# The experts' stage of a decoder layer, divided into 32 units and laid under a selective scan as a third chain

## The chip, the cores and the metric

The kernel runs on one core of one Trainium2 chip. The metric is the device time of one execution in microseconds (us). Everything is computed in float32. In the lines of the profile PE is TensorE (PEld its weight loads), DVE is VectorE, ACT is ScalarE, POOL is GpSimd and SP is SyncE, on whose queue all transfers are issued. L392 is line 392 of the kernel before.

## What is computed

One post-norm decoder layer on a batch of 32 sequences of 256 tokens of 256 features: a selective scan (Mamba), cross attention to a context with 16 heads of 16, and eight experts with gated feed-forward nets; after each a residual and a layer norm.

```python
x = layernorm(x + mamba(x))
x = layernorm(x + cross_attention(x, ctx))
x = layernorm(x + experts(x))

def mamba(x):
    xc, res = split(x @ W_in.T + b_in)                 # 512 and 512 channels
    u = silu(causal_conv3(xc) + conv_b)
    dlt, Bm, Cm = split(u @ W_x.T)                     # 64, 16, 16
    delta = softplus(dlt @ W_dt.T + b_dt)
    # in chunks of 64 tokens, for 512 channels x 16 states
    h[t] = exp(delta[t] * A) * h[t-1] + delta[t] * Bm[t] * u[t]
    y[t] = sum_n(h[t] * Cm[t])
    return (y * silu(res)) @ W_out.T + b_out

def experts(x):            # expert e has tokens 32 e .. 32 e + 31 of every sequence
    h = silu(x[e] @ w1[e]) * (x[e] @ w3[e])            # 256 -> 704
    return h @ w2[e]                                   # 704 -> 256
```

## The kernel before, and what sets its order

The work is done in two stages.

The first stage holds the scan and the attention of all 32 batches, in an order written out by hand: `tc.manual_schedule()` (L74) makes each engine execute its instructions in the order in which the Python code issues them. The main loop (L617 to L649) runs over steps. Sixteen steps make a batch (`NBLK`), each of 32 channels with 16 states; the 512 pairs of a step lie on 128 partitions and four rows of 256 tokens. The step number within the batch is called k here. A step consists of

- `load_step` (L326), the broadcast load of delta and delta times u for a step that lies `AHEAD` = 5 steps on;
- `decay` (L354), four exponentials on ACT, for the step after next, into one of three `da` buffers;
- `inject` (L368), one product on DVE into `bu`, with `b_bc`, which `spread_b` (L345) has PE write once a batch;
- `recur` (L378), the scan proper on DVE, into one of seven `h` buffers;
- `weigh` (L389), one product with C on POOL;
- after every fourth step `reduce` (L394), 32 matmul instructions on PE that sum over the states into `y`, and three steps later `gate` (L414) on DVE.

Between these, two chains run as Python generators, and `run` takes one of them on by one yield:

- `pre(b + 1)` (L224), called `nxt` in the loop: everything that the scan of the next batch needs. Transposes, `ps_in`, convolution, SiLU, `ps_x`, `ps_dt`, softplus (Abs, Relu, Exp and Ln on ACT, the rest on POOL), and the stores `dd` from which the steps load.
- `attn(b - 1)` (L420), called `prev`: output product of the scan, residual, norm, then the attention. Its parts are the scores `s` (L481) with 16 maxima on DVE (L495), `ps_m`, the subtraction of the maxima in `qT` (L507), the scores again in the other orientation with Exp (L564), `attend` (`ps_oT`, L522), `divide` (`ps_oB`, L540), output product `ps_o`, residual, norm, and the store into `x2d` in HBM. It begins at k=3 of the batch that follows its own.

All products of this stage take their place in PSUM from one pool of five banks, `bank` (L192). A product waits on the chip when its bank hasn't been read. Scores take four banks at once.

The second stage (L654 to L757) begins when the first has ended. Its order is not fixed by hand. It runs over the eight experts; the tokens of an expert from all 32 sequences are 1024 columns, taken in two halves of 512. For each half `up` (L686) forms w1 and w3 products, 512 columns wide, with SiLU on ACT from PSUM and the product on DVE; `down` (L708) forms the product with w2, residual, norm and store. Weights are loaded once for each expert, an expert ahead, into pools of two buffers. A float32 product is two matmul instructions in the profile.

Of the kernel before, what the change touches and what calls it, by code (L numbers as in the profile page):

```python
# [15 lines left out]
P = 128  # L16
# [12 lines left out]
AHEAD = 5  # L29
H, DK = 16, 16  # L30
NG = 4
E, FF = 8, 704
NFC = 6
CT = L // E
EPS = 1e-5
# [3 lines left out]
def decoder_kernel(ctx: ExitStack, tc: tile.TileContext, a: dict, out: bass.AP):  # L39
# [12 lines left out]
    def layernorm(pool, tiles):  # L52
# [7 lines left out]
        yield  # L60
        rstd = pool.tile([P, n, 1], F32, tag="ln_rstd", name="ln_rstd")
# [4 lines left out]
        nc.gpsimd.tensor_scalar_mul(off, off, -1.0)  # L66
        yield
# [5 lines left out]
    with ExitStack() as ph:  # L73
# [6 lines left out]
        esp = ph.enter_context(tc.tile_pool(name="esp", bufs=6))  # L80
        ldp = ph.enter_context(tc.tile_pool(name="ldp", bufs=AHEAD + 1))
        hp = ph.enter_context(tc.tile_pool(name="hp", bufs=7))
# [3 lines left out]
        ps_mm = ph.enter_context(tc.tile_pool(name="ps_mm", bufs=5, space=PSUM))  # L86
# [54 lines left out]
        b_v = column_v = wp.tile([P, 2, 1], F32, name="b_v")  # L141
# [49 lines left out]

        def bank(name):  # L192
            return ps_mm.tile([P, 2 * L], F32, tag="mm", name=name)
# [30 lines left out]
        def pre(b):  # L224

            ps = transposes(xs[b])
# [3 lines left out]
            nc.gpsimd.tensor_tensor(  # L230
                xs[b], xs[b], b_out.unsqueeze(1).to_broadcast([P, 2, D]), ALU.add
            )
# [10 lines left out]

            pss = [project(m2) for m2 in range(2)]
            yield
            for c in range(NDC):
                nc.scalar.activation(  # L247
                    xpad[:, c, 2:], pss[c // 2][:, c % 2], AF.Identity, bias=b_in[:, c : c + 1]
                )
            pss = [project(m2) for m2 in range(2, 4)]  # L250
# [3 lines left out]
            for c in range(NDC):  # L254
                m = NDC + c
                nc.scalar.activation(
                    sres[:, c, :], pss[c // 2][:, c % 2], AF.Identity, bias=b_in[:, m : m + 1]
                )
            pss = [
# [8 lines left out]

            nc.scalar.activation(sres, sres, AF.Silu)
            u = unit1.tile([P, NDC, L], F32, tag="u", name=f"u_{b}")  # L270
            for c in range(NDC):
                nc.scalar.activation(
                    u[:, c, :], pss[c // 2][:, c % 2], AF.Silu, bias=conv_b[:, c : c + 1]
                )
            yield
            ps = bank("ps_x")[:, :L]
# [7 lines left out]
            nc.scalar.copy(xp[:R], ps[:R])  # L284
            xps[b] = xp
            bcds[b] = bcd.tile([NS, L], F32, tag="bcd", name=f"bcd_{b}")
            nc.sync.dma_start(bcds[b], xp[DTR + NS : R])
            yield
            pss = [
# [10 lines left out]
            e = unit1.tile([P, NDC, L], F32, tag="e", name=f"ez_{b}")  # L300
            for dst, f in ((e, AF.Abs), (z, AF.Relu)):
                for c in range(NDC):
                    nc.scalar.activation(
                        dst[:, c, :], pss[c // 2][:, c % 2], f, bias=b_dt[:, c : c + 1]
                    )
            yield
            nc.scalar.activation(e, e, AF.Exp, scale=-1.0)
            lw = unit1.tile([P, NDC, L], F32, tag="lw", name=f"lw_{b}")
            nc.scalar.activation(lw, e, AF.Ln, bias=1.0)
            yield  # L310
            nc.gpsimd.tensor_tensor(z, z, lw, ALU.add)

            nc.gpsimd.tensor_scalar(lw, e, 1.0, -1.0, op0=ALU.add, op1=ALU.add)
            yield
            nc.gpsimd.tensor_tensor(e, e, lw, ALU.subtract)
            nc.gpsimd.tensor_tensor(z, z, e, ALU.add)
            yield
# [96 lines left out]
        def gate(i, y):  # L414
            b, c = i // NBLK, i % NBLK // NJ
            if c == 0:
                ygs[b] = unit1.tile([P, NDC, L], F32, tag="yg", name=f"yg_{b}")
            nc.vector.tensor_tensor(ygs[b][:, c, :], y, sress[b][:, c, :], ALU.mult)

        def attn(b):  # L420

            yg = ygs.pop(b)
            ctxT = cts.pop(b)
            ps_out = product(
# [21 lines left out]
            nc.vector.tensor_tensor(x1, ps_out, xs.pop(b), ALU.add)  # L446
            norm = layernorm(small, [x1[:, t, :] for t in range(2)])
            next(norm)
            kT = unit1.tile([P, NG, L], F32, tag="kT", name=f"kT_{b}")
            biased(kT, b_k, pss)  # L450
            yield
            next(norm)
            ps = product(
# [5 lines left out]
            next(norm, None)  # L459
            nc.scalar.copy(v[:, :, :, :DK], ps.rearrange("p t (h d) -> p t h d", d=DK))  # L460
            yield
# [4 lines left out]
            nc.gpsimd.tensor_tensor(x1, x1, b_o.unsqueeze(1).to_broadcast([P, 2, D]), ALU.add)  # L466
            yield
            pss = [project(w_q, x1T, g2) for g2 in range(2)]
            yield
            qT = unit1.tile([P, NG, L], F32, tag="qT", name=f"qT_{b}")  # L470
            biased(qT, b_q, pss)
            yield
# [18 lines left out]
            for g in range(NG):  # L491
                ss = scores(g, qT, kT)
# [3 lines left out]
            yield  # L496
# [8 lines left out]
            for g2, ps in enumerate(pss):  # L505
# [3 lines left out]
                )  # L509
            yield  # L510
            att = unit1.tile([P, 2, H, DK], F32, tag="att", name=f"att_{b}")
            HH = H // 2
            oT = None

            def attend(g, ess):

                nonlocal oT
                if g % 2 == 0:
                    oT = bank("ps_oT").rearrange("p (g n) -> p g n", g=2)
                for k in range(2):  # L520
                    for j in range(4):
                        nc.tensor.matmul(  # L522
                            oT[32 * j : 32 * j + 32, g % 2, :],
# [6 lines left out]
                        )  # L530

            def divide(g2, oT):

                oS = unit1.tile([P, 2, L], F32, tag="oS", name="oS")
                nc.scalar.copy(oS, oT)
                yield
                ps = bank("ps_oB").rearrange("p (t j n) -> p t j n", t=2, j=2)
                for t in range(2):
                    for j in range(2):
                        nc.tensor.transpose(  # L540
                            ps[:, t, j, :], oS[:, j, t * P : (t + 1) * P], ident
                        )
                yield
# [8 lines left out]
                )  # L552

            last, div = None, iter(())
            for g in range(NG + 1):
                if g < NG:
                    ss = scores(g, kT, qT)
                yield
                next(div, None)
                ess = []  # L560
                if g < NG:
                    for s in ss:
                        es = esp.tile([P, 2, L], F32, tag="es", name="es")
                        nc.scalar.activation(es, s, AF.Exp, scale=1.0 / DK**0.5)  # L564
                        ess.append(es)
                if last is not None:
                    attend(g - 1, last)
                    if g == 2:
                        div = divide(0, oT)
                last = ess  # L570
                yield
                next(div, None)
            for _ in div:
# [248 lines left out]
```

## Time and profile before

| | |
|---|---|
| time, median of 3 runs | 3479.11 us (3478.74 to 3484.37) |
| profiled execution | 3480.61 us, of which its span is 3478.9 us |
| PE busy | 2870.0 us, 82% of the span, 17284 matmuls |
| DVE busy | 2424.9 us, 70% |
| ACT busy | 1980.8 us, 57% |
| POOL busy | 1838.7 us, 53% |
| DMA | 377.10 MB, 108 GB/s over the span |
| mean granted clock of PE | 0.861 |

Busy time is the time in which an engine has an instruction under way. Matmuls are pipelined and their ends are modelled, so PE can be shown busy while it isn't at its peak. The granted clock is the share of the full PE clock that the chip allows at the time. An idle time is put down to the work whose end released the engine.

The costliest groups of the first stage are the product with C (L392, POOL, 512 times 2361 ns), the scan (L380, DVE, 512 times 2285 ns), the decays (L361, ACT, 2048 times 504 ns), `bu` (L371, DVE, 512 times 1222 ns) and the scores (L481, PE).

### The profile page before, as it was taken

What the parts mean: (1) busy time and instruction counts of PE and PEld (TensorE: products, weight loads), DVE (VectorE), ACT (ScalarE), POOL (GpSimd) and SP (SyncE); (2) the same over time, 40 slices, a digit from 0 to 9 for tenths busy, and PEclk for the clock granted to TensorE, in tenths of its full rate; (3) what the DMA queues carried; (4) which work ended last, traced back from release to release, by engine and by line L of the source; (5) the groups of instructions that cost most, each with busy time, mean ns of one, the idle gap of its engine ahead of it and who ended that gap; (6) DMA issues with size and microseconds to landing.
All of it is one profiled execution on the core that took longest, in us unless ns stands there. A gap on an engine that the chain in (4) does not pass through costs nothing. (4 is left out here: it accounts for less than half of the span.)

```text
span 3478.9 us, 47890 instructions
## 1 busy us (share of the span) xinstructions
PE 2870.0 (82%) x17284; PEld 1904.1 (55%) x17284; DVE 2424.9 (70%) x2447; ACT 1980.8 (57%) x4227; POOL 1838.7 (53%) x1143
## 2 busy tenths in 40 slices
PE   2378888888888888888888888888888787999998
PEld 2255555555555555555555555555555553555554
DVE  0578888888888888888888888888888872222222
ACT  1566666666666666666666666666666642121211
POOL 0666666666666666666666666666666640000001
PEclk9678888888888888888888888888888887999999
DMA  2554444444444444444444444444444422221320
GB/s 47 138 132 124 125 122 122 123 125 125 124 126 125 124 122 122 122 122 122 123 125 123 122 122 122 122 122 122 122 122 122 121 59 78 60 62 49 76 52 22
DMA packets 260158, 377.10 MB, mean 108 GB/s; under 512 B 34576, under 2 KB 123920, under 8 KB 259920
## 3 DMA queue, kind: packets, MB, share of 16 engines
q1 hardware_dynamic: 259920, 374.03, 39.5%
q8 instruction: 136, 2.23, 0.3%
q14 instruction: 102, 0.84, 0.1%
HBM read 323.08 MB, written 50.86 MB: 107 GB/s over the span
## 5 line engine op out<-in xcount | busy, mean ns | idle before, releaser
L392 POOL TENSOR_TENSOR h<-h,c_bc 128x1024 f32<-128x1024 f32 x512 | 1208.8, 2361 | 722.4 <-DVE h L380 645.1
L380 DVE TENSOR_TENSOR_SCAN h<-da,bu 128x1024 f32<-128x1024 f32 x512 | 1169.8, 2285 | 61.8 <-ACT da L361 6.3
L361 ACT ACTIVATE da<-ld,a_neg 128x252 f32<-128x252 f32 x2048 | 867.9, 504 | 534.7 <-DVE h L380 514.2
L371 DVE TENSOR_TENSOR bu<-ld,b_bc 128x1024 f32<-128x1024 f32 x512 | 625.6, 1222 | 58.4 <-DMA ld<-dd 49.3
L481 PE MATMUL s<-kT,qT 32*128 32x256 f32 x2048 | 401.1, 667 | 225.8 <-ACT qT L439 176.4
L495 DVE TENSOR_REDUCE mpad<-s 128x2 f32<-128x512 f32 x512 | 316.7, 681 | 280.0 <-PE s L481 280.0
L481 PEld LDWEIGHTS s<-kT,qT 32*128 32x128 f32 x2048 | 278.5, 310 | 338.0 <-ACT qT L439 188.9
L564 ACT ACTIVATE es<-s 128x512 f32<-128x512 f32 x512 | 270.5, 614 | 114.2 <-PE s L481 68.7
L62 POOL TENSOR_SCALAR ln_rstd<-ln_mv 128x2 f32<-128x2 f32 x96 | 21.8, 228 | 592.5 <-DVE ln_mv L59 589.9
L401 PE MATMUL y<-h,sel_y 128*32 128x256 f32 x4096 | 312.8, 453 | 22.9 <-POOL h L392 22.9
L481 PE MATMUL s<-qT,kT 32*128 32x256 f32 x2048 | 280.5, 454 | 43.4 <-ACT es L564 28.9
L705 DVE TENSOR_TENSOR h_ff<-sg,pu 128x512 f32<-128x512 f32 x96 | 65.9, 686 | 294.6 <-PE pu L696 294.6
L217 PE MATMUL ps_in<-xT,w_in 128*128 128x256 f32 x1024 | 243.8, 393 | 24.6 <-ACT xT L229 24.6
L481 PEld LDWEIGHTS s<-qT,kT 32*128 32x128 f32 x2048 | 169.9, 206 | 165.8 <-ACT es L564 106.6
L401 PEld LDWEIGHTS y<-h,sel_y 128*32 128x32 f32 x4096 | 142.8, 128 | 166.5 <-issue 89.4
L217 PEld LDWEIGHTS ps_in<-xT,w_in 128*128 128x128 f32 x1024 | 193.8, 194 | 70.2 <-ACT xT L229 32.7
L716 PE MATMUL po<-w,h_ff 128*128 128x256 f32 (+1 forms) x768 | 193.0, 396 | 0.0
L704 ACT ACTIVATE sg<-pg 128x512 f32<-128x512 f32 x96 | 57.2, 596 | 235.4 <-PE pg L696 235.4
L217 PE MATMUL ps_conv<-xpad,taps 128*128 128x256 f32 x768 | 173.0, 381 | 21.5 <-ACT xpad L247 21.5
L696 PE MATMUL pg<-x2T,w 128*128 128x512 f32 (+1 forms) x384 | 182.1, 596 | 0.0
L696 PE MATMUL pu<-x2T,w 128*128 128x512 f32 (+1 forms) x384 | 180.4, 592 | 0.0
L522 PE MATMUL ps_oT<-es,v 128*32 128x256 f32 x2048 | 154.9, 424 | 24.1 <-ACT es L564 24.1
(100 smaller groups left out, 3786.1 us busy)
## 6 DMA issues: line engine op xcount, KB each, us to landing
ld<-dd SPq DMA_DIRECT2D x1024, 256.0 KB, 4.1
dd<-delta SPq DMA_DIRECT2D x32, 512.0 KB, 2.9
dd<-u SPq DMA_DIRECT2D x32, 512.0 KB, 3.2
w<-in_w SPq DMA_DIRECT2D x16, 704.0 KB, 4.8
x<-in_x SPq DMA_DIRECT2D x32, 256.0 KB, 4.2
c_bc<-bcd SPq DMA_DIRECT2D x64, 128.0 KB, 3.4
ctxT<-in_ctxT SPq DMA_DIRECT2D x32, 256.0 KB, 4.7
x2d<-x SPq DMA_DIRECT2D x32, 256.0 KB, 2.1
```

Of the source, the lines that this page charges most:

```text
L217: nc.tensor.matmul(ps[:, j, :], l, r, start=(k == 0), stop=(k == len(terms) - 1))
L361: nc.scalar.activation(da[:, g, q].rearrange("p (k t) -> p k t", t=CHUNK)[:, :, 1:], loads[i][:, 0, g].rearrange("p (k t) -> p k t", t=CHU ...
L371: nc.vector.tensor_tensor(bu, loads.pop(i)[:, 1].unsqueeze(2).to_broadcast([P, GB, NQ, L]), b_bcs[i // NBLK].unsqueeze(1).to_broadcast([P, ...
L380: nc.vector.tensor_tensor_scan(h.rearrange("p g q t -> p (g q t)"), das_of.pop(i).rearrange("p g q t -> p (g q t)"), bus.pop(i).rearrange( ...
L392: nc.gpsimd.tensor_tensor(hs[i], hs[i], c_bc, ALU.mult)
L401: nc.tensor.matmul(y[32 * j : 32 * j + 32, :], sel_y[:, g, :], hs[i - NJ + 1 + j][:, g, q, :], start=(g == 0 and q == 0), stop=(g == GB - ...
L481: nc.tensor.matmul(ss[j][:, t, :], left[r : r + 32, g, t * P : (t + 1) * P], right[r : r + 32, g, :], start=True, stop=True,)
L495: nc.vector.tensor_reduce(mpad[:, :, g, 32 * j + DK], s, AX.X, ALU.max)
L522: nc.tensor.matmul(oT[32 * j : 32 * j + 32, g % 2, :], v[:, k, 4 * g + j, :], ess[j][:, k, :], start=(k == 0), stop=(k == 1), tile_positio ...
L564: nc.scalar.activation(es, s, AF.Exp, scale=1.0 / DK**0.5)
L696: nc.tensor.matmul(ps[:m], w[:, k, f * P : f * P + m], x2T[:, k, cols], start=(k == 0), stop=(k == 1),)
L716: nc.tensor.matmul(ps[:, j, :], h[:m, f, t * P : (t + 1) * P], w2[:m, f, :], start=(f == 0), stop=(f == NFC - 1),)
```

## The change

The second stage is removed. Its work is divided into 32 units, each of four sequences and two experts, 128 tokens for each expert: unit u takes sequences 4 (u // 4) to 4 (u // 4) + 3 and experts 2 (u % 4) and 2 (u % 4) + 1. The units run one after the other in a generator, `units`, which the main loop takes on as a third chain, twice in each step (`expert_step`). Unit u begins when its four sequences are stored in `x2d` and the loop has reached step 6 of batch u + 5 (`LAG`). What is left after the last step runs behind the loop, alternating with the last attention.

A unit loads `xe` (tokens of both experts) and the first expert's w2, transposes, and forms the w1 products for both experts in three banks of four tiles of 704 / 128; ACT copies them into `h`. Then it loads w3 into the buffers that held w1, and yields `HOLD`: it is taken on only by the call in `pre` just ahead of the SiLU there, so that its own SiLU, over all of `h` in SBUF, stands beside that one. The w3 products follow, with a product on DVE for each bank, then `ps_down` with w2 of the first expert, the load of the second expert's w2 into the same buffer and of the next unit's w1, the second half of `ps_down`, residual, norm and store.

`live`, `take` and `done` count the banks of PSUM while the order is made: a chain that wants banks yields until that many of five are not in use in the order so far, instead of issuing a product that would wait on the chip.

```diff
-AHEAD = 5
+AHEAD = 4
+HBUFS = 6
+RING = 5
+GE = P // CT
+UNITS = B // GE * (E // 2)
+LAG = 5
...
+        def take(n):
+            nonlocal live
+            while live + n > RING:
+                yield
+            live += n
+        def done(n):
+            nonlocal live
+            live -= n
...
+            expert_step(True)
             nc.scalar.activation(sres, sres, AF.Silu)
...
+        def load_w13(u, which, e):
+            t = fw.tile([P, 2, FF], F32, tag="w13", name=f"{which}_{u}_{e}")
+            src = a[which][2 * (u % 4) + e].rearrange("(k p) f -> p k f", p=P)
+            nc.sync.dma_start(t, src)
+            w13s[u, which, e] = t
...
+        def expert_unit(u):
+            yield
+            yield
+            xe = xes.pop(u)
+            yield from take(1)
+            ps = bank("ps_xe").rearrange("p (k e n) -> p k e n", k=2, e=2)
+            for k in range(2):
+                for e in range(2):
+                    nc.tensor.transpose(ps[:, k, e, :], xe[:, e, k * P : (k + 1) * P], ident)
+            yield
+            x2T = unit1.tile([P, 2, 2, P], F32, tag="x2T", name=f"x2T_{u}")
+            nc.scalar.copy(x2T, ps)
+            done(1)
+            yield
+            def hidden(which, b):
+                ps = bank("ps_h").rearrange("p (i n) -> p i n", i=4)
+                for i in range(4):
+                    e, f = FS[4 * b + i]
+                    m = min(P, FF - f * P)
+                    for k in range(2):
+                        nc.tensor.matmul(
+                            ps[:m, i, :],
+                            w13s[u, which, e][:, k, f * P : f * P + m],
+                            x2T[:, k, e, :],
+                            start=(k == 0),
+                            stop=(k == 1),
+                        )
+                return ps
...
+            for b in range(3):
+                yield from take(1)
+                ps = hidden("w1", b)
+                yield
+                for m, i, j in parts(b):
+                    nc.scalar.copy(h[:m, 4 * b + i : 4 * b + j, :], ps[:m, i:j, :])
+                done(1)
+                yield
+            for e in range(2):
+                load_w13(u, "w3", e)
+            yield HOLD
+            nc.scalar.activation(h[:, :FULL, :], h[:, :FULL, :], AF.Silu)
+            nc.scalar.activation(h[:REST, FULL:, :], h[:REST, FULL:, :], AF.Silu)
+            yield
+            for b in range(3):
+                yield from take(1)
+                ps = hidden("w3", b)
+                yield
+                yield
+                for m, i, j in parts(b):
+                    at_ = h[:m, 4 * b + i : 4 * b + j, :]
+                    nc.vector.tensor_tensor(at_, at_, ps[:m, i:j, :], ALU.mult)
+                done(1)
+            yield from take(1)
+            po = bank("ps_down").rearrange("p (e n) -> p e n", e=2)
+            for e in range(2):
+                terms = [i for i in range(len(FS)) if FS[i][0] == e]
...
+                yield
+                if e == 0:
+                    load_w2(u, 1)
+                    if u + 1 < UNITS:
+                        for ee in range(2):
+                            load_w13(u + 1, "w1", ee)
+                    yield
+            nc.vector.tensor_tensor(xe, po, xe, ALU.add)
+            done(1)
+            for _ in layernorm(small, [xe[:, e, :] for e in range(2)]):
+                yield
+            yield
+            for e in range(2):
+                nc.sync.dma_start(rows_of(out, u, e), xe[:, e, :])
+
+        def units():
+            for u in range(UNITS):
+                while stored <= u // 4 * GE + GE - 1 or i < (u + LAG) * NBLK + 6:
+                    yield
+                load_xe(u)
+                load_w2(u, 0)
+                yield from expert_unit(u)
...
+        def expert_step(on_hold=False):
+            nonlocal held
+            if held == on_hold:
+                held = next(unit, None) is HOLD
```

The main loop, after the change, in its new parts:

```diff
             run(prev)
+            expert_step()
             if i < STEPS:
+                if len(hs) == HBUFS:
+                    drain(sums)
                 recur(i)
             run(nxt)
             run(prev)
             if i < STEPS:
                 weigh(i)
-            for f in later.pop(i, ()):
-                f()
+            run(sums)
             if i % NJ == NJ - 1 and i < STEPS:
-                at(i + 2, lambda i=i: summed(i))
-            run(prev if k % 2 else nxt)
-            if k == 3 and b:
-                for _ in prev:
-                    pass
+                drain(sums)
+                sums = summed(i)
+            if b == LAG and k == 0:
+                for e in range(2):
+                    load_w13(0, "w1", e)
+            expert_step()
+            run(prev)
+            if k % 2 == 0:
+                run(nxt)
+                run(prev)
+            if b + 1 == B and k == 3:
+                expert_step(True)
+            if k == 4 and b:
+                drain(prev)
                 prev = attn(b - 1)
-        for _ in prev:
-            pass
+        i = 10**6
+        for _ in unit:
+            run(prev)
```

In the two old chains `take` and `done` stand around every product, and steps are moved apart: `layernorm` yields twice where it yielded once, `pre` issues the residual's bias on POOL a step later, Abs and Relu alternate, and softplus is done in two halves in buffers of half the size (`halves`). The scores, the second scores together with `attend`, and `divide` are each a step of their own; `oT` takes a bank for each group of four heads and is copied in four halves. Attention begins at k=4 instead of k=3. Room in SBUF comes from `AHEAD` 4, six `h` buffers (`HBUFS`), four `es` instead of six, and buffers that are shared (`oS` and `aT` use that of `x1T`, the second residual is written over `x1`); `yg` has two buffers.

## The prediction

> **What bounds the kernel now.** The profiled execution took 3480.61 us, its span 3478.9, so 1.7 us lie around the span; the median of the runs is 3479.11. I make the sum against the span. First I read the busy time by stretches (bounds, length, then busy us of PE, its weight loads, DVE, ACT, POOL; granted clock, DMA share, GB/s), to part the scan from the experts' stage.
>
> ```profile
> 176.00:2728.00 2552.00, 2122.87 (x14356) 1486.03 (x14356) 2118.64 (x1997) 1725.95 (x3726) 1647.54 (x916) 0.85 0.45 123
> ...
> 2920.00:3479.00 559.00, 541.66 (x1664) 285.43 (x1664) 119.06 (x256) 109.90 (x193) 43.51 (x128) 0.99 0.23 59
> ```
>
> The scan is not full on any engine: PE 83%, DVE 83%, ACT 68%. The experts' stage is PE alone at full clock. The batches' `b_bc` products (L349) start at 81.1 us for the first and 2771.5 for the last, that is 86.8 a batch; from 1992.11 to 2770.63 nine batches took 86.5 each.
>
> Next the timeline of one batch. DVE (start, duration, group):
>
> ```profile
> 1512.26 2.29 DVE L380 TENSOR_TENSOR_SCAN h<-da,bu 128x1024 f32<-128x1024 f32 x1
> ...
> 1523.47 2.49 DVE L495 TENSOR_REDUCE mpad<-s 128x2 f32<-128x512 f32 x4 [8.92 <-PE s L481]
> ...
> 1539.67 1.26 DVE L507 TENSOR_TENSOR qT<-qT,ps_m 128x512 f32<-128x512 f32 x2
> ```
>
> Scans and their `bu` follow without a gap until 1514.55; then DVE stands 8.9 us before the reduction of the first scores. PE in the same batch:
>
> ```profile
> 1511.76 3.72 PE L217 MATMUL ps_qk<-x1T,w_q 128*128 128x256 f32 x16 [0.68 <-ACT x1T L465]
> ...
> 1521.36 6.13 PE L481 MATMUL s<-kT,qT 32*128 32x256 f32 x34 [5.88 <-ACT qT L439]
> ...
> 1562.02 0.44 PE L208 MATMUL ps_tr<-ident,att 128*128 128x128 f32 x2 [1.89 <-DVE att L547]
> ...
> 1576.92 5.35 PE L217 MATMUL ps_conv<-xpad,taps 128*128 128x256 f32 x24
> ...
> 1582.10 3.62 PE L217 MATMUL ps_out<-w_out,yg 128*128 128x256 f32 x16
> ...
> 1585.56 3.62 PE L217 MATMUL ps_qk<-ctxT,w_k 128*128 128x256 f32 x16
> ```
>
> PE has the queries at 1515.5, and the scores begin only at 1521.36, after a stop of 5.9 us. Then PE works nearly without a pause from 1562 (transposes of `att`) to the next queries. ACT says why the scores wait:
>
> ```profile
> 1514.46 1.11 ACT L307 ACTIVATE ez<-ez 128x1024 f32<-128x1024 f32 x1
> ...
> 1515.60 1.28 ACT L309 ACT_TABLE_LOAD   x1
> ...
> 1520.86 1.54 ACT L439 ACTIVATE qT<-ps_qk,b_q 128x256 f32<-128x256 f32 x4
> ```
>
> `qT` is behind softplus and its tables. The granted clock in short windows (the column after POOL) is what the stop costs afterwards:
>
> ```profile
> 1516.00:1520.00 4.00, 0.00 (x0) 0.00 (x0) 0.00 (x0) 3.96 (x5) 1.98 (x1) 0.79 0.00 0
> ...
> 1520.00:1524.00 4.00, 2.64 (x18) 2.08 (x18) 0.53 (x1) 3.97 (x11) 3.91 (x2) 0.50 0.00 0
> ...
> 1562.00:1566.00 4.00, 3.98 (x12) 3.27 (x13) 3.78 (x3) 2.28 (x5) 2.10 (x2) 0.58 0.69 192
> ...
> 1582.00:1586.00 4.00, 4.00 (x21) 3.51 (x20) 2.58 (x3) 3.97 (x7) 2.68 (x2) 1.00 0.15 35
> ```
>
> **What the skill says.** "TensorE: Matmul & The Clock Gate", Part 1, says that an idle window of about 3.4 us halves the PE clock and a busy one of that length restores it: the trace agrees, 1.00 at 1582 and 0.50 after the stop at 1516. So denser PE work can't be priced at the stage's mean clock; I price it at full clock. The same page, Back-to-back issue gap, gives a warm matmul N/2.4 ns + 2.5: the trace has 24 `ps_conv` instructions from 1576.92 to 1582.10, 216 ns each at N=256 (a float32 product is two instructions), which is twice 106.7, and 2.5 (two passes). For N=128, which no float32 product has here, the same form gives 109 ns. "Trainium Kernel Development and Optimization", Performance Expectations, warns that PE busy time misleads; so I count instructions. "ScalarE: Activation LUTs", What ACT_TABLE_LOAD costs, says that each change of set costs a load: 1283 ns in this trace; the diff puts the experts' SiLU beside the existing one, so no load is added under the scan.
>
> **The change part by part.**
>
> *Order.* I walked the loop with pencil: every yield, and the count of five banks. One unit goes through in each batch, without a slip: its transposes at step k=11, three w1 banks at k=13, 14 and 15, w3 banks at k=3, 4 and 5 of the next batch, `ps_down` at k=6 and 7, residual at k=8. Units 0 to 25 lie wholly under the scan; unit 26 is held before its SiLU and ends behind the scan, with 27 to 31. So batches 0 to 4 carry nothing, batch 5 half a unit, 26 batches (6 to 31) a whole one.
>
> *PE work of a unit.* The moving operand of w1 and w3 is 128 wide instead of 512: 24 products, 48 instructions each for w1 and w3. The two rows for bounds:
>
> ```profile
> L696 PE MATMUL pg<-x2T,w 128*128 128x512 f32 x320 | 151.2, 595 | 0.0
> ...
> L217 PEld LDWEIGHTS ps_in<-xT,w_in 128*128 128x128 f32 x1024 | 193.8, 194 | 70.2 <-ACT xT L229 32.7 <-issue 12.3
> ```
>
> By columns an instruction takes 109 ns (512 wide: 429 ns from start to start in the stage's timeline, a quarter is 107); if its 128 weights can't be hidden, 190. I take 150: 7.2 us for w1, 7.2 for w3. Down: 24 instructions x 216 = 5.2. Four transposes 0.7. Together 20.3 us, 16.4 to 24.1.
>
> *Other engines.* DVE per unit: two products of 0.69, two halves of 0.42, residual 0.69, statistics 1.2: 4.1 us on 71.6 (2118.64/2552 x 86.3). ACT: copies of w1 0.6 x 3, `x2T` 0.6, SiLU 1.35 and 0.45 in place, norm 1.2: 5.4. POOL: norm 1.4, and more, shorter softplus instructions, on 55.7. None becomes full, provided the order lets them run.
>
> *Does it fit beside the old work?* Each engine runs in program order, so I cut a batch at the places where one engine waits for the other.
>
> A, from the transposes of `att` until `ps_down` is through. Before, PE needs 39.4 us from 1562.02 to the end of the queries (1515.5 + 86). In the new order PE has here: transposes 0.5, `ps_in` 6.9, `ps_o` 1.7, two `y` 3.8 (1.9 each), conv 5.2, `ps_x` 1.7, out and k 6.9, dt and v 3.5, transposes 0.5, queries 3.5 = 34.2; and 7.2 of w3 and 5.2 of down: 46.6. Stops: `ps_x` waits for u, now behind one table load and 1.8 us of the experts' SiLU, with only one w3 bank to fill the 2.4 us that remain; `x1T` is behind v, Abs/Relu and a decay on ACT, 2.7; the clock is half after PE's wait for `att`, 1.7 (1562:1566 shows 0.58). 53.4 us. The gap before the scores goes: ACT has `qT` by then; what is late next is PE itself. DVE has only 8 steps of 3.6 us and some 8 us more to do here, and waits for `ps_o`, `ps_out`, w3 and at last for `ps_down`, whose residual is queued ahead of scan 8 and all reductions.
>
> B, from there to the subtraction in `qT`: DVE. Residual and statistics 1.9, three scans 6.9, two `bu` 2.4, 16 reductions 9.9 (2.48 per four), gate 0.4, wait for `ps_m` 1.2, subtraction 1.3 = 24.0 us. PE has nothing of the experts here, though it would have time.
>
> C, from there to the next transposes of `att`: a chain of PE and ACT. Scores 4 x 1.35, `ps_oT` 4 x 1.07, expert transposes 0.7, w1 7.2, `ps_oB` 1.3, `y` 1.9, `b_bc` 0.9 = 21.7; then `bu`, scan, reciprocal, product on DVE 4.2, since `b_bc` is behind the last `ps_oB` and DVE's next step behind `b_bc`; hops 1.5. 27.4 us.
>
> A + B + C = 104.8, I take 105 (86.5 before). Without the unit the same sums give 41 + 22 + 23.4 (DVE bound: six steps), about 87 as in the trace, so I take 87 for batches 0 to 4 and 93 for batch 5. Bounds of one batch: 98 with 109 ns, no stop and a warm clock, and B and C at DVE's own pace plus hops; 112 with 190 ns and with `xe` late: its load is queued on SP behind the store of softplus, which waits for POOL, and behind the store of the unit before; landing 5.2 us, and PE stands with the scores of attention behind it. I take nothing for that; 5 is the other end.
>
> *Loads.* w1, w3 and w2 of a unit, 3.5 MB, each wait on SP for a buffer that PE frees. The steps' loads stand behind them, four ahead instead of five, at 3.6 us a step and 4.1 to land: no cost; without that cover some 2 us a batch. Six `h` instead of seven: scan k waits for the `y` four to six steps back; inside A and C. Merged buffers, wider `yg`: nothing, their readers are done earlier.
>
> *The tail.* Before, attention of the last batch runs alone from 2853.52 to 2914.2: 61 us; then come 565 of experts, which go. After: the last sums 7; attention with the rest of unit 26 and unit 27, whose 30 us of PE, two waits for weights and one for `xe` are in the same queue: 105. Units 28 to 31 need the last `x2d` and run one by one, each exposed: `xe` 5.2, transposes and copy 1.5, w1 7.2, load of w3 (its two buffers are w1's) 6, w3 7.2, product 1, down 5.2, wait for the second w2 5, residual and norm 5, store 1.7, hops 2: 47. Together 7 + 105 + 188 = 300 (230 to 340).
>
> *Sum.* 81 + 5 x 87 + 93 + 26 x 105 + 300 = 3639; with the 1.7 around it 3641, I say 3640. It breaks even at 98.8 us a batch.
>
> **Rivals.** *R1, forecast:* the unit's PE work adds itself to A and C, 3640. For it: PE's dense run from 1562 to 1601, and that B takes no expert work.
>
> *R2, faster:* PE's idle and half-clock time takes the unit. Mechanism: w3 and down fill PE where it stood before the scores, so the clock stays full and A has no stops. For it: 60 us of warm PE work in 86.5 by count, and 0.50 clock for 20 us a batch. Against: in-order queues, A's 46.6 without a stop. At 93 a batch, 81 + 435 + 88 + 26 x 93 + 290 = 3312; it decides below 98.8.
>
> *R3, far slower:* 128 weights aren't hidden and `xe` is late: 112 a batch, 3822.
>
> *R4:* the units slip and pile up behind the scan: each slip moves 47 us out and takes 18 from a batch. Against: the pencil count. Ten slips: near 3900.
>
> **Numbers.** R1 0.60, R2 0.22, R3 0.14, R4 0.04. R1's own range is 3490 to 3760 (batches from 100 to 109, tail 250 to 330), with a little of it at or under the present time. The range takes in the slower half of R2 and most of R3: 3400 to 3800. A measurement tells 0.2% (7 us) from no change. Faster 0.23, same 0.03, slower 0.74.
>
> **What would show it.** The starts of `b_bc` from batch 6 on: 105 apart, under 98.8 proves me wrong. DVE waiting for `ps_down` and `ps_out` in each batch, and no longer for the first scores. Clock above 0.9. 48 instructions of w1 in 7.2 us. The last units about 47 us apart. PE waiting for `xe` before its transposes would be R3.

## The result, and the profile after

The changed kernel takes 4213.67 us (4202.22 to 4223.92), 1.211 times the kernel before, with a 95% interval of 1.207 to 1.214. The forecast was 3640 in a range of 3400 to 3800: slower, as forecast, but far more so, 735 us instead of 161. The profiled execution has a span of 4222.1 us.

The starts of `b_bc` (L388 in the changed kernel) part it into the terms of the forecast's sum:

| part | forecast, us | measured, us |
|---|---|---|
| to the first `b_bc` | 81 | 80.6 |
| batches 0 to 5 | 5 x 87 + 93 = 528 | 611.3 |
| batches 6 to 30 | 25 x 105 = 2625 | 3131.9, that is 125.3 each |
| batch 31 and all behind it | 105 + 300 = 405 | 398.4 |
| sum | 3639 | 4222.1 |

So the last row comes out within 7 us, the batches with a unit are 20 us too short each, and already the batches without one are too short: 2, 3 and 4 take 102 us, not 87.

Busy time says nothing of this. From the page after: PE has more to do and is busy for a smaller share, and its granted clock in the fortieths of the span (PEclk, in tenths, the page after and then the page before) is no better than before.

```profile
PE 3087.7 (73%) x19588; PEld 2186.0 (52%) x19588; DVE 2431.0 (58%) x2479; ACT 2064.3 (49%) x4457; POOL 1860.1 (44%) x1271
...
PEclk8677778778888877788777788777788877778876
```

```profile
PEclk9678888888888888888888888888888887999999
```

The waits of the changed kernel say where the time is (engine and line, waited for whom: us in total, times, longest):

```profile
...
DVE rec L601 <- PE ps_oB L594: 529.3, 33, 21.2
...
PE ps_xe L701 <- DMA xe<-x2d: 423.5, 59, 13.9
...
DVE xe L775 <- PE ps_down L761: 358.6, 32, 12.8
ACT es L622 <- PE ps_oT L577: 228.8, 95, 5.4
```

The second line is new: PE stands in front of the experts' transposes until the load of `xe` has landed. DVE's wait for `ps_oB`, 26.0 us in the kernel before, and ACT's for `ps_oT`, 45.3 there, are behind it or beside it. One batch on PE, the one that begins at 2188:

```profile
2193.82 0.69 PE L230 MATMUL ps_tr<-ident,att 128*128 128x128 f32 x2 [3.69 <-DVE att L602]
...
2218.01 1.95 PE L715 MATMUL ps_h<-x2T,w 128*128 128x128 f32 x16
2219.79 3.62 PE L239 MATMUL ps_out<-w_out,yg 128*128 128x256 f32 x16
...
2245.63 2.95 PE L761 MATMUL ps_down<-w,h 128*128 128x256 f32 x12
2248.51 1.56 PE L535 MATMUL s<-kT,qT 32*128 32x256 f32 x18
...
2270.07 2.09 PE L535 MATMUL s<-qT,kT 32*128 32x256 f32 x16 [0.23 <-DVE qT L564]
2284.79 0.45 PE L701 MATMUL ps_xe<-ident,xe 128*128 128x128 f32 x1 [12.62 <-DMA xe<-x2d]
2288.73 0.90 PE L701 MATMUL ps_xe<-ident,xe 128*128 128x128 f32 x3 [3.50 <-DMA xe<-x2d]
2289.56 2.09 PE L535 MATMUL s<-qT,kT 32*128 32x256 f32 x16
...
2321.13 0.69 PE L230 MATMUL ps_tr<-ident,att 128*128 128x128 f32 x2 [3.69 <-DVE att L602]
```

These lines give the three parts of the forecast's batch. A, from the transposes of `att` (2193.82) to the end of the second `ps_down` (2248.58): 54.8 us, against 53.4. B, to the end of the subtraction (2270.61, a line of DVE): 22.0 against 24.0. C, to the next transposes of `att` (2321.13): 50.5 against 27.4. As means of the batches 10 to 30 they are 54.6, 22.1 and 49.0. So the whole of the missing time is in C. The reader should see the two gaps of 12.62 and 3.50 us in C: one for each half of `xe`, with only one transpose between them, and the scores, `ps_oT` and w1 queued behind. Why the load is late stands on the queue of SP:

```profile
2268.76 0.37 SPq L358 DMA_DIRECT2D dd<-delta  x1
2273.38 0.37 SPq L360 DMA_DIRECT2D dd<-u  x1
...
2275.39 1.29 SPq L781 DMA_DIRECT2D out<-xe  x2
2280.40 1.14 SPq L688 DMA_DIRECT2D xe<-x2d  x2
```

The load of `xe` stands behind a row of others: the two stores of `dd` wait for POOL's softplus, two loads of `c_bc` (left out here) and the store of the unit before stand behind them, and the load waits 3.7 us more until that store has left the only `xe` buffer. PE uses the second half of it 8.3 us after its issue.

DVE in the same stretch is what makes the wait cost a batch its length:

```profile
2281.58 1.23 DVE L410 TENSOR_TENSOR bu<-ld,b_bc 128x1024 f32<-128x1024 f32 x1
2303.25 0.26 DVE L601 RECIPROCAL rec<-ps_oB 128x16 f32<-128x16 f32 x1 [20.44 <-PE ps_oB L594]
```

Between 2282.8 and 2303.25 DVE executes nothing: `rec` waits for `ps_oB`, which PE has behind all this, and the scans are queued behind `rec`.

And the batches without a unit, here batch 3, PE first and then ACT:

```profile
454.39 5.80 PE L535 MATMUL s<-qT,kT 32*128 32x256 f32 x32 [0.23 <-DVE qT L564]
460.13 1.94 PE L577 MATMUL ps_oT<-es,v 128*32 128x256 f32 x16
462.79 3.54 PE L535 MATMUL s<-qT,kT 32*128 32x256 f32 x16 [0.73 <-ACT es L622]
466.25 1.93 PE L577 MATMUL ps_oT<-es,v 128*32 128x256 f32 x16
```

```profile
456.50 2.06 ACT L622 ACTIVATE es<-s 128x512 f32<-128x512 f32 x4 [3.73 <-PE s L535]
...
462.14 2.06 ACT L622 ACTIVATE es<-s 128x512 f32<-128x512 f32 x4 [1.91 <-PE ps_oT L577]
...
468.26 2.07 ACT L622 ACTIVATE es<-s 128x512 f32<-128x512 f32 x4 [3.80 <-PE ps_oT L577]
...
479.11 2.06 ACT L622 ACTIVATE es<-s 128x512 f32<-128x512 f32 x4 [5.37 <-PE ps_oT L577]
```

From the second group on, the scores, `ps_oT` and Exp follow each other strictly. The Exp of a group (four instructions) begins 5.6, 6.1 and 10.9 us after that of the group before, though the four take only 2.06, and ACT names `ps_oT` as what it waited for. There are only four `es` buffers, so ACT may not write group g before PE has read group g - 1; and on PE that reading stands behind the scores of group g.

The last four units, alone behind the scan, are 49 to 50 us apart, with 12.6 to 13.9 us of waiting for `xe` in front of each, a gap of 4 for w3 and one of 4.8 for the second w2. 48 instructions of 128 columns take 7.13 us. That is 149 ns each as a mean, but no instruction takes it: the granted clock is 0.51 in the first 3 us of the 7.13 and 1.00 in the next 3, and from start to start the instructions are 214 ns apart in the first part and 111 in the second. (16 of them, from 2218.01 to 2219.79 in the batch above, at a clock of 1.00, are 111 ns apart too.)

```profile
4077.68 0.45 PE L701 MATMUL ps_xe<-ident,xe 128*128 128x128 f32 x1 [13.78 <-DMA xe<-x2d]
...
4081.10 7.13 PE L715 MATMUL ps_h<-x2T,w 128*128 128x128 f32 x48 [0.68 <-ACT x2T L704]
4092.15 8.35 PE L715 MATMUL ps_h<-x2T,w 128*128 128x128 f32 x48 [3.93 <-DMA w<-in_w]
...
4108.31 4.52 PE L761 MATMUL ps_down<-w,h 128*128 128x256 f32 x12 [4.83 <-DMA w<-in_w]
4126.50 0.45 PE L701 MATMUL ps_xe<-ident,xe 128*128 128x128 f32 x1 [13.67 <-DMA xe<-x2d]
```

### The profile page after: what moved, and what is told of

It is laid out like the page before. It is cut to its first block, busy times and chain, and to the rows that moved or that the text cites. A ratio compares the mean times of both kernels' runs of the same rounds, so it can differ in the third digit from the quotient of the medians.

```text
span 4222.1 us, 53083 instructions
## 1 busy us (share of the span) xinstructions
PE 3087.7 (73%) x19588; PEld 2186.0 (52%) x19588; DVE 2431.0 (58%) x2479; ACT 2064.3 (49%) x4457; POOL 1860.1 (44%) x1271
## 4 chain that ended last, share of the span: by engine, by line
PE 50%; DVE 19%; ACT 11%; DMA 9%; issue 8%; SPq 2%; POOL 1%; DVEq 0%; ACTq 0%; POOLq 0%
PE ps_h L715 8%; DVE mpad L550 7%; DVE h L419 7%; PE ps_qk L239 7%; PE s L535 6%; PE ps_oT L577 5%; PE ps_in L239 5%; PE ps_down L761 5%; PE y L440 4%; DMA xe<-x2d 4%; ACT da L400 4%; DMA out<-xe 3%; DVE bu L410 3%; ACT es L622 3%; PE ps_out L239 3%
## 5 line engine op out<-in xcount | busy, mean ns | idle before, releaser
L715 PE MATMUL ps_h<-x2T,w 128*128 128x128 f32 (+1 forms) x3072 | 446.6, 304 | 41.1 <-ACT es L622 22.0
L715 PEld LDWEIGHTS ps_h<-x2T,w 128*128 128x128 f32 (+1 forms) x3072 | 410.2, 206 | 110.6 <-issue 50.2
L622 ACT ACTIVATE es<-s 128x512 f32<-128x512 f32 x512 | 264.4, 602 | 347.2 <-PE ps_oT L577 228.8
L535 PE MATMUL s<-kT,qT 32*128 32x256 f32 x2048 | 303.7, 533 | 97.2 <-DVE mpad L550 97.1
L701 PE MATMUL ps_xe<-ident,xe 128*128 128x128 f32 x128 | 42.2, 435 | 425.6 <-DMA xe<-x2d 423.5
L239 PE MATMUL ps_in<-xT,w_in 128*128 128x256 f32 x1024 | 310.4, 471 | 2.7 <-ACT xT L252 2.7
L535 PE MATMUL s<-qT,kT 32*128 32x256 f32 x2048 | 285.9, 558 | 35.6 <-ACT es L622 22.1
L535 PEld LDWEIGHTS s<-kT,qT 32*128 32x128 f32 x2048 | 190.5, 252 | 209.4 <-DVE mpad L550 176.6
L239 PEld LDWEIGHTS ps_in<-xT,w_in 128*128 128x128 f32 x1024 | 245.4, 246 | 62.2 <-issue 12.3
L577 PE MATMUL ps_oT<-es,v 128*32 128x256 f32 x2048 | 226.0, 489 | 27.0 <-ACT es L622 21.8
L239 PE MATMUL ps_qk<-x1T,w_q 128*128 128x256 f32 x512 | 175.7, 518 | 91.4 <-ACT x1T L515 91.4
L775 DVE TENSOR_TENSOR xe<-ps_down,xe 128x512 f32<-128x512 f32 x32 | 22.1, 692 | 358.6 <-PE ps_down L761 358.6
```

What stands on the lines that cost most here:

```text
L239: nc.tensor.matmul(ps[:, j, :], l, r, start=(k == 0), stop=(k == len(terms) - 1))
L535: nc.tensor.matmul(ss[j][:, t, :], left[r : r + 32, g, t * P : (t + 1) * P], right[r : r + 32, g, :], start=True, stop=True,)
L577: nc.tensor.matmul(oT[32 * j : 32 * j + 32, :], v[:, k, 4 * g + j, :], ess[j][:, k, :], start=(k == 0), stop=(k == 1), tile_position=(0, 3 ...
L715: nc.tensor.matmul(ps[:m, i, :], w13s[u, which, e][:, k, f * P : f * P + m], x2T[:, k, e, :], start=(k == 0), stop=(k == 1),)
```

## The experiments

Ratios are to the kernel before, timed beside each run, with 95% intervals. A batch's parts A, B and C are means of the batches 10 to 30; A is taken to end at the first scores.

**e1, a resident tile instead of `xe`.** What is PE's wait worth?

```diff
-nc.tensor.transpose(ps[:, k, e, :], xe[:, e, k * P : (k + 1) * P], ident)
+nc.tensor.transpose(ps[:, k, e, :], w_in[:, e, k * P : (k + 1) * P], ident)
```

> The experts' four transposes read a resident tile (two slices of w_in) instead of xe, so PE doesn't wait for the load of xe; the load itself, the residual and every other instruction and its place stay. The hidden products are then formed from weights of w_in instead of tokens[...]. Theory L (PE stands for the load of xe, 16 to 17 us in each of 26 batches and 13 before each of the last units): 4214 - 26 x 16 - 5 x 13 = about 3730 (3680 to 3800). Rival P (the 20 us of PE work of a unit are what makes the batch long, the wait only takes the place of another): not below 4100.

4041.13 us, 1.163 (1.161 to 1.165): 173 less, neither the 484 of theory L nor the nothing of rival P. A batch goes from 125 to 120. The products with w1 keep their price, 111 ns an instruction at full clock. The waits of this run show what came in place:

```profile
ACT da L400 <- DMA ld<-dd: 266.3, 28, 11.9
...
PE ps_h L715 <- ACT es L622: 228.8, 28, 11.0
```

The decays now wait for the steps' loads, up to 11.9 us at a time, and PE's products with w1 wait for the Exp of the same late ACT, 28 times and 228.8 us in all. On SP the load of `xe` still waits for the store of the unit before, and the steps' loads are queued behind it. So the transfer was late for two users, and only one of them was freed. Whether the fifth step of lead that the change took from these loads (`AHEAD`) would have covered them was not run.

**e4, `xe` loaded earlier.**

```diff
-            xes[u] = unit1.tile([P, 2, D], F32, tag="xe", name=f"xe_{u}")
+            xes[u] = unit2.tile([P, 2, D], F32, tag="xe", name=f"xe_{u}")
...
                         for ee in range(2):
                             load_w13(u + 1, "w1", ee)
+                        if stored > (u + 1) // 4 * GE + GE - 1:
+                            load_xe(u + 1)
                     yield
...
-                load_xe(u)
+                if u not in xes:
+                    load_xe(u)
                 load_w2(u, 0)
```

> Two xe buffers, and the load of the next unit's xe is issued with its w1, in the middle of ps_down of the unit before, instead of behind that unit's store. Nothing is left out. Theory L: the wait of PE in front of the transposes goes, as with a resident tile: 3680 to 3800; the last four units lose some 13 us each too. Rival Q (the transfers themselves are late in the queue of SP, wherever they are issued): above 3950.

3949.63 us, 1.137 (1.134 to 1.139): 264 less. The wait of PE for `xe` is no longer among the long ones, a batch takes about 116, and 3949.63 lies just below the 3950 above which rival Q had put it. Theory L's own size fails too: it asked for 3800 at most. C goes from 49.0 to 40.1, while A stays at 53.8. So the load is a real cause and not the only one. The decays still wait 150.9 us for `ld` in this run, and `bu` 150.0 for `b_bc`; what else is left needs another cause, which the batches without a unit show alone.

**e2 and e3, without experts.** In e2 `units()` gives nothing and the second norm is stored as the output. In e3, beside that:

```diff
-        esp = ph.enter_context(tc.tile_pool(name="esp", bufs=4))
+        esp = ph.enter_context(tc.tile_pool(name="esp", bufs=8))
...
-                yield from take((4 if g < NG else 0) + (1 if g else 0))
                 if g < NG:
+                    yield from take(4)
                     ss = scores(g, kT, qT)
-                if g:
-                    oT = attend(g - 1, last)
                 yield
                 ess = []
                 if g < NG:
                     for s in ss:
                         es = esp.tile([P, 2, L], F32, tag="es", name="es")
                         nc.scalar.activation(es, s, AF.Exp, scale=1.0 / DK**0.5)
                         ess.append(es)
                     done(4)
                 if last is not None:
+                    yield from take(1)
+                    oT = attend(g - 1, last)
+                yield
+                if last is not None:
...
                     nc.scalar.copy(oS[:, (g - 1) % 2, :], oT)
                     done(1)
                 last = ess
-                yield
```

> The experts are left out: no unit is built, the second norm is stored as the output; both old chains, the scan and the loop stay as in the changed kernel. Theory O (the new order of the two old chains costs about 15 us a batch by itself, as the batches 2 to 4 of the changed kernel show with 102 us): 32 batches of 102, start 81 and the last attention 65: about 3400. Rival S (the first batches are only slow at the start, or for the weights of later): batches of 87, about 2930, as the first stage of the kernel before (its experts begin at 2914).

> The same without experts, and eight es buffers, with Exp of a group issued ahead of ps_oT of the group before it (as the kernel before does) instead of behind. Theory E (four es buffers chain scores, ps_oT and Exp of each group, 5.6 to 10.8 us from one to the next): 5 to 8 us a batch less than without experts as it stands, about 3200. Rival K (the place of divide, of b_bc and of y in the order sets the pace): within 60 us of that run.

e2: 3390.18 us, 0.976 (0.974 to 0.977): 100 to 103 us in nearly every batch, so theory O holds. Without any experts the new order takes nearly as long as the whole kernel before, whose first stage was through at 2914. e3: 2985.37 us, 0.859 (0.858 to 0.861), 405 less than e2, 88 to 90 a batch: theory E, and more than it asked. All of it is in C: 33.7 us in e2 and 20.6 in e3, with A at 48.7 and 49.0 and B at 19.2 in both. Exp in e3:

```profile
429.48 2.06 ACT L620 ACTIVATE es<-s 128x512 f32<-128x512 f32 x4 [3.73 <-PE s L535]
...
433.11 2.03 ACT L620 ACTIVATE es<-s 128x512 f32<-128x512 f32 x4
...
437.14 2.06 ACT L620 ACTIVATE es<-s 128x512 f32<-128x512 f32 x4 [1.66 <-PE s L535]
...
443.08 2.07 ACT L620 ACTIVATE es<-s 128x512 f32<-128x512 f32 x4 [0.46 <-PE s L535]
```

They come 3.6 to 5.9 us apart, with decays between them.

**e5 and e6, buffers or order.** e5 is e2 with eight `es` buffers alone, e6 is e2 with the order of e3 alone.

> Without experts as in e2, eight es buffers, and the order as in the changed kernel (Exp of a group issued behind ps_oT of the group before it). Theory B (it is the number of buffers: with four, ACT's Exp must wait on the chip until ps_oT has read them, and ps_oT stands behind the next scores on PE): most of the gain of e3, 2990 to 3100. Rival R (it is the order, five banks asked for at once by scores and ps_oT together, so that the steps come later): 3300 to 3400.

> Without experts, four es buffers, and Exp issued ahead of ps_oT as in e3. Theory B: at least 3250, since the Exp of a group still waits for the four buffers. Rival R: 2990 to 3100.

e5: 3135.52 us, 0.902 (0.900 to 0.904), 94 a batch. e6: 3226.25 us, 0.928 (0.926 to 0.930), 96 a batch. The buffers alone give 255 of the 405 us, the order alone 164: the two nearly add up, and neither theory alone is right. Both results lie between the ranges of the two theories.

**e7 and e8, both causes with all experts in.** Six `es` buffers and Exp ahead of `ps_oT`, room from one `yg` buffer; e8 has the `xe` of e4 too.

> Nothing is left out: the changed kernel with six es buffers and Exp ahead of ps_oT (room from one yg buffer instead of two). If what e3 showed (12.7 us a batch) holds with the units too: 4214 - 32 x 12.7 = about 3810. Rival W (with the units PE stands for xe in the same place, and the gain of the buffers is lost in that wait): above 4050.

> The same with two xe buffers and the early load of e4: both causes taken out. If they add: 3950 - 32 x 12.7 = about 3540. Rival V (the units' own PE work and the steps' loads then set the pace at 105 us a batch, as forecast): about 3640. Faster than before only if a batch comes under 99 us.

e7: 4137.12 us, 1.190 (1.188 to 1.192), only 77 less: rival W. Its waits still have 415 us of PE for `xe`:

```profile
DVE rec L601 <- PE ps_oB L594: 569.3, 37, 21.7
...
PE ps_xe L702 <- DMA xe<-x2d: 415.5, 60, 13.7
```

e8: 3746.0 us, 1.078 (1.076 to 1.080), 468 less than the changed kernel, where the two alone give 264 and 77. They are one behind the other in the same part of the batch, C: 49.0 in the changed kernel, 47.9 in e7, 40.1 in e4, 34.0 in e8. With the late `xe` left, most of the gain of the order is waited away (77 us, against 204 from e4 to e8); with the order left, a third of the gain of `xe` (264, against 391 from e7 to e8). A batch takes 109, near the 105 that the forecast gave for a unit without these two waits. Rival V is nearer than addition, but the run is 106 us above it too.

**e9 to e12, what sets the pace then.** In e8 DVE still waits 355.7 us for `ps_down`, whose residual is queued ahead of a scan and all reductions. e9 is e8 with `ps_down` later:

```diff
+            for _ in range(2):
+                yield
             yield from take(1)
             po = bank("ps_down").rearrange("p (e n) -> p e n", e=2)
...
-                    yield
+                    for _ in range(3):
+                        yield
             nc.vector.tensor_tensor(xe, po, xe, ALU.add)
```

The last of these edits stands between the two halves of `ps_down`. e10 has seven `es` buffers (one `xp` and one `ctxT` buffer instead of two, the context loaded at step 8), e11 is e9 and e10 together, and e12 is e10 with four yields behind the experts' SiLU instead.

> e8 with two more yields ahead of each half of ps_down, so that on PE the first half stands behind the queries and the second between the third and the fourth scores, where PE waits for DVE, and DVE's residual behind the reductions. Nothing is left out. Theory D (DVE's wait of 12 us a batch for ps_down is the tail of PE's run from the transposes of att; what moves out of that run comes off the batch): 5 us a batch, 3746 - 26 x 5 = about 3616. Rival G (ps_down then delays scores or the next transposes as much): 3710 to 3800.

> e8 with seven es buffers instead of six, room from one xp and one ctxT buffer, the context of a batch loaded at step 8. Without experts eight buffers give 88.7 us a batch and six 95.6 in batches 2 to 4 of e8. Theory B: half of that with seven, 3 us a batch, about 3660. Rival: with a unit in each batch PE and not ACT sets the pace of that part: 3730 or more.

> Both: e10 with the yields of e9. If they add, about 3530; faster than before (3475) only if a batch comes under 99 us.

> e10 with four more yields behind the experts' SiLU, so that w3 as well as ps_down stand later on PE (first w3 bank behind ps_out, last behind the queries, ps_down between the scores). Theory D: a little less than e11, 3500; rival: w3 then stands in front of the first scores again, 3560 or more.

| run | us | ratio (95%) | a batch with a unit | A | B | C |
|---|---|---|---|---|---|---|
| e8 | 3746.0 | 1.078 (1.076 to 1.080) | 109 | 53.2 | 22.1 | 34.0 |
| e9 | 3494.63 | 1.0035 (1.0024 to 1.0046) | 99.0 | 53.3 | 21.8 | 23.9 |
| e10 | 3694.28 | 1.061 (1.059 to 1.063) | 105 to 112 | 54.0 | 22.1 | 32.1 |
| e11 | 3387.26 | 0.973 (0.971 to 0.975) | 95.6 | 51.6 | 21.9 | 22.1 |
| e12 | 3557.02 | 1.022 (1.020 to 1.025) | 101 to 104 | 55.9 | 23.0 | 23.5 |

e9 gains 251 us, 10 a batch where theory D asked for 5, but not in the way of theory D. Only one half of `ps_down`, 2.6 us, leaves PE's run ahead of the first scores, and A doesn't become shorter, for other work takes its place there. DVE's wait for `ps_down` goes from 355.7 to 91.4, but its wait for the first scores goes from 47.0 to 234.6. The gain is in C. The added yields move everything of the unit that follows, so the next unit's transposes and w1 come later as well. In e8 the first w1 bank stands between the third scores and the `ps_oT` of the second group, and all three banks ahead of `b_bc` and the transposes of `att`; in e9 the first comes behind the fourth scores, and the third and `b_bc` behind the transposes, that is in A. First e8, then e9:

```profile
3035.28 3.83 PE L535 MATMUL s<-qT,kT 32*128 32x256 f32 x16
3039.05 3.77 PE L716 MATMUL ps_h<-x2T,w 128*128 128x128 f32 x16
3042.74 1.07 PE L577 MATMUL ps_oT<-es,v 128*32 128x256 f32 x16
```

```profile
3028.01 1.95 PE L716 MATMUL ps_h<-x2T,w 128*128 128x128 f32 x16
3029.79 0.60 PE L230 MATMUL ps_tr<-ident,att 128*128 128x128 f32 x4
3030.23 2.08 PE L716 MATMUL ps_h<-x2T,w 128*128 128x128 f32 x16
3032.23 1.13 PE L388 MATMUL b_bc<-xp,sel_b 80*128 80x256 f32 x4
```

ACT's wait for `ps_oT` goes down too, from 230.4 to 94.9. The half of `ps_down` that left A stands in B, which doesn't become longer by it.

Seven buffers alone give 52, on top of e9 107: e10 lies between its two theories, and e11 is 56 us below the sum of e9 and e10. e12 moves more work and gains less: C is 23.5, near that of e9, but its w3 banks come behind `ps_out` and around the queries, still ahead of the first scores, and A is 55.9. With 3557 it is at the edge of its rival's 3560. In e11 PE takes one half of `ps_down` among the scores, where it used to wait for DVE:

```profile
1755.50 3.86 PE L535 MATMUL s<-kT,qT 32*128 32x256 f32 x16 [0.60 <-DVE mpad L550]
1759.29 4.63 PE L764 MATMUL ps_down<-w,h 128*128 128x256 f32 x12
1763.86 1.15 PE L535 MATMUL s<-kT,qT 32*128 32x256 f32 x16
```

e11 beats both kernels: 2.7% faster than the one before.

## Why the prediction was wrong

*Direction right, A and B right in size.* PE's dense run from the transposes of `att` takes the unit's work in line, 54.8 us against 53.4, and DVE's next step waits for `ps_down`. B was right within 2 us. The order of the units, counted by hand, is that of the trace.

*What came out right by offsets.* The price of an instruction of 128 columns, taken between two bounds at 150 ns, was too high: it is 111 at full clock, and only the half clock in front made 48 of them take 7.13 us. The profile before had such instructions: the four transposes of `x` at 1566.57 are 109 ns apart. In A, w3 took 5.8 us instead of 7.2, while the first half of `ps_in`, at half clock after PE's wait for `att`, took 2.8 us more than at full clock, where 1.7 was taken. The last row of the table has batch 31 with the others' 20 us too few, so the 300 of the tail was some 27 too long (an estimate: 398.4 less 125.3 is 273). And that e9, with 99.0 us a batch, lies on the break-even of 98.8 holds only because its batches 0 to 5 took 576 us instead of 528 and what follows batch 31 some 258 instead of 300. Two slips changed nothing: a unit's weights are 4.3 MB (six times 704 KB), not 3.5, and the last `b_bc` before starts at 2770.63.

*The step that failed, first: part C, and there the load of `xe`.* The prediction had the mechanism, placed "behind the store of softplus, which waits for POOL, and behind the store of the unit before", and then wrote "I take nothing for that; 5 is the other end". It is 12.6 + 3.5 = 16.1 us in the batch shown, and 423.5 in the run. The bound of 5 was the landing alone; the wait for the store, though named, and the second half had no price, and nothing had excluded them. The sum for the tail did price the same chain, residual and norm 5, store 1.7, `xe` 5.2 and hops 2, and the gaps there measured 12.6 to 13.9. Under the scan it was taken at nothing. Of the other 7 us of C in that batch the scores and `ps_oT` account for most: some 16 us instead of 9.7, with a granted clock of 0.50 from 2284 to 2292 and from 2296 to 2300, after the stop. e4 shows that at least 264 us hang on it, e7 that with the wait in place hardly anything else can be gained.

*Second: the same part without a unit.* "Without the unit the same sums give 41 + 22 + 23.4 (DVE bound: six steps), about 87 as in the trace". The parts were 49.0, 19.2 and 34.2 in batch 3. That the sum came out as the old 86.5 was taken as support, but the old trace had another order, and e3, which does take 88.7, has 49.0, 19.2 and 20.6: the sum met it with A 8 us too short and B and C too long. Six `es` buffers had become four and Exp had moved behind `ps_oT`: neither was priced at all. The Trainium skill says of a gap that repeats on the engine that should be saturated, in Perfetto Trace Analysis, Optimization Strategy, that there may not be enough SBUF or PSUM for the next tile, and names the buffer count. Here it is ACT, busy for 49% of the span, that waits, up to 5.37 us for `ps_oT` in batch 3, and the 255 us of e5 show that the buffer count was a cause. The prediction put the shared buffers together as "nothing". e2 shows 102 us a batch without any experts, e3 that the two edits make 405 us of it, e5 and e6 that both count. In part A without a unit PE waits 6.9 us for `x1T`, where 2.7 was taken and 2.3 is measured with a unit. The prediction had subtracted the unit's PE work from A with a unit; the wait grows when that work is gone, so it can't simply be subtracted.

*Third, in a smaller way: "no cost" for the steps' loads.* It held in the changed kernel only while PE's own wait covered it. When that goes and the queue stays, as in e1, the decays wait for `ld`, 266.3 us; in e4, whose `xe` is loaded earlier, 150.9, and in e8 29.0.

*A sign that failed.* "Clock above 0.9" was to show the steps right: it is 0.797, under the 0.861 of before, though PE has more to do. PE waiting for `xe` was named as the sign of R3, and it came.

*Rivals.* R3 named `xe` but put its end at 112 a batch, for it priced the wait at 5; its other cause, weights that can't be hidden, isn't seen at 111 ns an instruction. R2, PE's work in the time when PE waits, failed in the order given; e11 comes to 95.6 a batch with half of `ps_down` where PE had waited for DVE, w1 behind the scores, and the two causes above taken out.

What stays open: how the remaining 95.6 us of e11 divide between PE and the chain of Exp, and how much of the gain of e9 in C is due to the place of w1, of `b_bc` and of the residual; no run parted them.

## What to carry to other kernels

In queues that run in program order, price the wait of a moved or added instruction together with everything queued behind it, and follow a load through its own queue: what stands ahead of its issue, which store must leave its buffer, when its last half lands. A buffer count that is cut to make room is an edit of its own and belongs in the sum, above all where the producer and the reader of the buffer alternate. Put new work where the engine waits for another, which the timeline of the batch shows, not where it is already the run that others wait for. Read the price of an instruction from start to start at one granted clock, not from a group that spans two. And when a run confirms the size of a theory, look whether the time left the part that the theory named.

## What was not expected of the hardware

A store of two times 128 KB issued at 2275.39 and 1.29 us long on the queue released its buffer for the next load at 2280.40, and PE used the two parts of that load 4.4 and 8.3 us after its issue. A float32 instruction with 128 weights and 128 columns starts 111 ns after the one before it at a granted clock of 1.00, and 214 ns after it at 0.50; the 190 that the prediction took for a weight load that can't be hidden doesn't show at full clock. And more PE work did not raise the granted clock by itself: 0.797 in the changed kernel, 0.866 in e9 and 0.892 in e11, with the same PE work. PE's stops of more than 3 us are 104 in the changed kernel, 700 us in all, and 24 and 23 in e9 and e11, some 155 us in each; the difference between the last two is not explained by them.
